# Neural-operator attention block on one core: scores in four column groups, grams in blocks, another row basis, softmax by batch, and pinned ends of the load stage

## The chip, the cores and the metric

The kernel runs on one core of a Trainium2 chip. The metric is device time in microseconds of that core for one execution. Before the change three runs gave 870.6, 871.68 and 877.57, median 871.68. One further execution was profiled and took 871.11; its recorded span is 869.6.

## The reference

The input x has 4 batches of 32 tokens; each token is an image of 128x128 fp32. The network has two layers. Layer 0 adds to x an attention over Fourier operators of the row-normalised x (`_L0_conv_ref`), then a recurrent scan; layer 1 is a resampling convolution and another scan. The change touches the start of layer 0 only:

```python
x = x + _L0_conv_ref(_ln_c(x), ...)
# in _L0_conv_ref: 16 heads; every token is one image
k = fno_layer(tokens_norm, key_w, key_skip_w, key_skip_b, (64, 64))
q = fno_layer(tokens_norm, query_w, query_skip_w, query_skip_b, (64, 64))
v = fno_layer(tokens_norm, value_w, value_skip_w, value_skip_b, (128, 128))
dprod = softmax(einsum('bhtd,bhsd->bhts', qf, kf) / scale, axis=-1)
attn = einsum('bhts,bhsd->bhtd', dprod, vf)
attn = fno_layer(attn, proj_w, proj_skip_w, proj_skip_b, (H, W))
```

`fno_layer` is a 1x1 convolution resampled through the Fourier domain plus a product with 16x9 (or 32x17) complex Fourier weights. Within a batch the scores are thus a sum of two parts: products of few Fourier coefficients with weights by head, and for all heads the same inner products of the images resampled to 64x64 (the grams), scaled by query_skip_w * key_skip_w of the head. Because attention is linear in v, the kernel mixes images with one 32x32 matrix per batch, and Fourier coefficients with the probabilities by head.

## The kernel before

All 128 images stand in on-chip memory as `XA`, 128 rows in the partitions, (batch, token, column) in the free dimension. The stage that loads and transforms them works in eight steps k of 16 images, two per batch.

- `stats(k, n)` takes mean and variance of each image row (L824, one instruction per image) and small vectors from them (L382 to L387, `rsqrt_of` with a square root on ACT, L830, L832). L833 fills `rv4`, from which the scale `s4` of a token's own norm comes later.
- `transform(k)` normalises the images in place (L846 on ACT for 10 of 16, L848 on DVE for 6), multiplies each with 130 constant columns (L863, `ps_st`, three images to a PSUM tile of which there are two), and copies the result to `A1` (L865 on DVE for the first and fourth of six groups, L867 on ACT for the others). Of the 130 columns 64 are a row Fourier transform and 66 resample the rows from 128 to 64: 64 real ones and two imaginary ones. Then come the column transform (L874, `ps_pf`, four groups of 32 output partitions) and the column resampling (L883, `ps_pr`, two groups of 64; the real and the imaginary part are each 512 wide), which ACT copies to `Rn` (L885). Last, L887 issues on SP the write of the 16 normalised images to a DRAM scratch, `normed`.
- `scores(b)` takes a batch's coefficients (L894 `FF`, L895 its transpose, L901 `ps_fr` copies them to all partition groups, L902 `Frep`), multiplies by head (L915, L929, L930 `KM`), transposes (L923 `ps_fq`, L937 `ps_kt`, copies L925 and L938) and multiplies (L941) into `psc`, batch b in partitions 32b to 32b+31, all 16 heads side by side in 512 columns.
- `grams(k)` (L951, `pg`) sums 32 products of 64x64 for two batches at once; of the result only the two diagonal 32x32 blocks are read (L1011).
- `weights()` and `filters()` prepare parameters; they are generators, as the others are, and a loop takes one step of each between two groups of `ps_st`. `filters` tests and stores the taps of layer 1's filters (L760 to L806 on DVE, L770 and L771 `ps_f` on PE, L749 and L808 write `hankel` in DRAM, which L1945 reads much later).

The loop over k (below) sets in which order the work is written out. Outside a block `in_order()` a planner may still place each engine's instructions otherwise; inside one, the order written is each engine's order.

After the loop, SP reads the scratch back with rows and images exchanged (L983, eight parts of 1 MB), and one softmax follows for all batches: `Pm` holds 16 heads x 32 tokens in 512 columns for the 128 (batch, token) partitions (L1022 to L1031), four transposes (L1035), scaling to `PTs` (L1036, L1038), and the sum over heads to the mixing matrix `CTbd` (L1044 to L1053). POOL clears `YT` (L1249).

The next stage is pinned by the list `SUMS`: F (L1261, `df`) multiplies coefficients on DVE, Y (L1274, `ps_y`) sums them with `PTs` on PE, M (L1067, `pm`) mixes images with `CTbd`.

## Time and profile before

| stretch (us) | what runs | length | PE busy | DVE busy | ACT busy |
|---|---|---|---|---|---|
| 20:40 | transforms 0 and 1, most input | 20 | 18.12 | 18.22 | 14.24 |
| 40:60 | transforms 2, 3, scores of batch 0 | 20 | 18.77 | 17.28 | 13.02 |
| 60:80 | transforms 3, 4, first grams | 20 | 19.66 | 18.57 | 13.77 |
| 80:100 | transforms 5, 6 | 20 | 18.86 | 13.09 | 12.83 |
| 130:140 | softmax | 10 | 2.13 | 8.89 | 1.26 |
| 140:150 | sums and mixing | 10 | 10.00 | 10.00 | 6.47 |

Time of the profiled execution 871.11, its span 869.6. Over the whole span PE is busy 88%, DVE 82%, ACT 74%, POOL 42%; the chain that ended last lies on PE for 39%, DVE 22%, ACT 13%.

To read it: a busy share says how long an engine had an instruction in flight. Matmul ends are modelled and overlap, so the share of PE is no measure of its speed. A releaser is what ended an engine's idle time. Engines are PE (matmul), PEld (its weight load), DVE (vector), ACT (scalar), POOL (GpSimd), SP (issues transfers).

### The profile page before, as it was taken

The page shows a single profiled execution, that of the slowest core. Times are in us where ns is not written, and L with a number is a line of the kernel's source. Part 1 is how long each engine was busy: PE and PEld are TensorE (multiplying, and loading weights), DVE is VectorE, ACT ScalarE, POOL GpSimd, SP SyncE. Part 2 cuts the span into 40 slices and gives each one's busy share as a digit, 9 for nine tenths or more (in the row PEclk, how much of TensorE's full clock was granted, in tenths as well). Part 3 has the DMA queues.
Part 4 walks back from the last instruction along what each step waited for, and adds up shares of the span by engine and source line. Part 5 has one row for each costly group of instructions (what it writes and reads, how often), then busy time and mean ns, then how long its engine had stood idle before and what let it go on. Part 6 is the DMA issues. An engine that isn't in the chain of part 4 may idle for free.

```text
span 869.6 us, 30563 instructions
## 1 busy us (share of the span) xinstructions
PE 762.7 (88%) x12326; PEld 559.4 (64%) x12326; DVE 712.0 (82%) x2322; ACT 640.2 (74%) x1647; POOL 364.2 (42%) x604
## 2 busy tenths in 40 slices
PE   1999996986878999899779979999999999998994
PEld 1656553335644655645339968888788887875993
DVE  5987749977588899899889988977868877678996
ACT  2765743585728698989779977877777887777994
POOL 2000000011435445364410016788788786972263
PEclk9999997996689899999999979999999999999997
DMA  9955991259711011120000000111111101118554
GB/s 216 265 159 116 256 368 68 101 220 265 191 50 49 26 44 31 49 73 26 25 1 1 1 3 17 41 41 39 29 40 28 41 28 41 35 44 288 175 197 137
DMA packets 105128, 83.18 MB, mean 96 GB/s; under 512 B 5457, under 2 KB 98129, under 8 KB 102865
## 3 DMA queue, kind: packets, MB, share of 16 engines
q1 hardware_dynamic: 104641, 80.86, 31.0%
q8 instruction: 99, 1.62, 0.8%
q0 software_dynamic: 288, 0.01, 0.2%
q14 instruction: 52, 0.43, 0.2%
q10 hardware_dynamic: 48, 0.26, 0.2%
HBM read 47.46 MB, written 33.66 MB: 93 GB/s over the span
## 4 chain that ended last, share of the span: by engine, by line
PE 39%; DVE 22%; ACT 13%; POOL 8%; issue 5%; SPq 0%; DVEq 0%; ACTq 0%; POOLq 0%
PE ps_k L2043 5%; PE ps_d L2173 4%; DVE XA L1562 4%; ACT WXY L1892 4%; DVE XA L1561 4%; PE ps_scan L1890 4%; ACT yw L1892 3%; PE pm L1067 3%; PE ps_st L1404 3%; PE ps_r L2043 2%; POOL XN L2022 2%; PE ps_e L2180 2%; PE ps_inv L488 2%; PE ps_y L1274 2%; PE ps_w L2119 2%
## 5 line engine op out<-in xcount | busy, mean ns | idle before, releaser
L2163 DVE SCALAR_TENSOR_TENSOR U<-raw 128x512 f32<-128x512 f32 x128 | 90.2, 733 | 27.7 <-ACT raw L2155 27.5
L1891 DVE SCALAR_TENSOR_TENSOR ps_scan<-WXY,bs,ps_scan 128x128 f32<-128x128 f32 x376 | 104.7, 351 | 1.2 <-PE ps_scan L1890 0.8
L2043 PE MATMUL ps_k<-WXY,q 64*64 64x134 f32 x2048 | 85.7, 280 | 1.3 <-issue 0.4
L2155 ACT COPY raw<-ps_k 128x512 f32<-128x512 f32 x128 | 71.2, 599 | 17.8 <-PE ps_k L2043 15.1
L2173 PEld LDWEIGHTS ps_d<-WXY,U 128*64 128x64 f32 x2048 | 66.7, 137 | 19.3 <-issue 11.4
L2022 POOL TENSOR_SCALAR XN<-XA,c_r,c_o 128x128 f32<-128x128 f32 x120 | 75.8, 642 | 4.7 <-issue 2.2
L2022 POOL TENSOR_SCALAR xn<-XA,f_r,f_o 128x128 f32<-128x128 f32 x120 | 68.3, 579 | 17.7 <-PE ps_x L2043 11.7
L2173 PE MATMUL ps_d<-WXY,U 128*64 128x67 f32 x2048 | 73.3, 224 | 1.2 <-ACT q L2186 0.9
L2043 PEld LDWEIGHTS ps_k<-WXY,q 64*64 64x64 f32 x2048 | 60.2, 134 | 7.1 <-DVE U L2163 0.8
L2043 PE MATMUL ps_r<-WXY,XN 64*64 64x134 f32 x1024 | 58.6, 287 | 3.0 <-DVE XN L2022 1.3
L863 PE MATMUL ps_st<-cst,XA 128*128 128x130 f32 x256 | 44.1, 310 | 16.6 <-ACT XA L846 13.0
L863 PEld LDWEIGHTS ps_st<-cst,XA 128*128 128x128 f32 x256 | 35.2, 204 | 30.3 <-ACT XA L846 14.4
L1619 ACT ACTIVATE xn<-XA,f_o,f_r 128x128 f32<-128x128 f32 x120 | 51.0, 489 | 4.6 <-DVE f_o L1601 3.4
L1398 ACT ACTIVATE Z<-Z,k,aB 128x128 f32<-128x128 f32 x128 | 51.1, 481 | 4.2 <-DVE Z L1393 4.0
L1561 DVE SCALAR_TENSOR_TENSOR XA<-ps_inv,r1B,xin 128x128 f32<-128x128 f32 x128 | 44.0, 344 | 8.2 <-PE ps_inv L1554 8.2
L1562 DVE SCALAR_TENSOR_TENSOR XA<-Z,gB,XA 128x128 f32<-128x128 f32 x128 | 46.3, 362 | 5.0
L2002 POOL TENSOR_TENSOR c_r<-c_e,neg_half 128x16 f32<-128x16 f32 (+2 forms) x10 | 25.7, 2565 | 52.9 <-DVE c_e L1995 52.7
L2141 ACT COPY q<-ps_r 128x512 f32<-128x512 f32 x64 | 38.3, 599 | 12.2 <-PE ps_r L2043 11.8
L503 PE MATMUL ps_inv<-invq,cst 64*128 64x512 f32 x128 | 41.4, 674 | 3.9 <-ACT invq L494 3.2
L453 PE MATMUL ps_wx<-xt,wvt 128*128 128x512 f32 x64 | 35.8, 643 | 6.5 <-ACT WXY L460 5.2
L2180 PE MATMUL ps_e<-WXY,q 128*64 128x67 f32 x1024 | 41.1, 222 | 0.0
L1890 PE MATMUL ps_scan<-y,wvt 128*128 128x128 f32 x246 | 40.5, 281 | 0.0
(442 smaller groups left out, 2102.4 us busy)
## 6 DMA issues: line engine op xcount, KB each, us to landing
XA<-in_x_dram SPq DMA_DIRECT2D x16, 512.0 KB, 7.5
normed<-XA SPq DMA_DIRECT2D x8, 1024.0 KB, 7.3
XA<-normed SPq DMA_DIRECT2D x8, 1024.0 KB, 16.0
mixed<-XA SPq DMA_DIRECT2D x8, 1024.0 KB, 3.9
XA<-mixed SPq DMA_DIRECT2D x32, 256.0 KB, 5.3
xin<-in_x_dram SPq DMA_DIRECT2D x32, 256.0 KB, 3.2
turned<-XA SPq DMA_DIRECT2D x32, 256.0 KB, 2.5
out_dram<-res SPq DMA_DIRECT2D x52, 128.0 KB, 2.1
```

Of the source, the lines that this page charges most:

```text
L863: mm(p[:, i, :], XA[:, b, t0 + j + i, :], cst[:, C_E : C_E + 130], start=True, stop=True)
L1561: stt(a, p2[c, b][:, i], r1B[:, j : j + 1], xin[c, b - b % 2][:, b % 2, i], ALU.mult, ALU.add)
L1562: stt(a, Z[c][:, b, i], gB[c][:, n : n + 1], a, ALU.mult, ALU.add)
L1890: mm(p4, self.t[:, 1, :], prev, start=True, stop=True)
L1891: stt(p4, WX[:, :, h, :], s[:, 0:1], p4, ALU.mult, ALU.add)
L1892: nc.scalar.activation(dst, p4, AF.Sigmoid, bias=s[:, 1:2])
L2022: e.tensor_scalar(dst, src_, r, o, ALU.mult, ALU.add)
L2043: m = mm(dst, data, taps, start=(n == 0 and (i, j) not in last), stop=(n == 1), skip_group_check=True)
L2155: nc.scalar.copy(raw[u, k], banks["k", u][:, k])
L2163: stt(U[u][:, k].rearrange("p k s m -> p (k s m)"), v, SLOPE, v, ALU.mult, ALU.max)
L2173: mm(p[HALVES[s], m, b, REACH[k]], U[v][:, b, k, s, HALVES[m]], DR[:, k, REACH[k]], start=(m == 0 and b == 0 and k == 0), stop=(k == 1), s ...
L2180: mm(p[HALVES[j], b * P : b * P + P][:, REACH[m]], q3[v - 1][:, m, b, HALVES[j]], DC[:, m, REACH[m]], start=(b == 0 and m == 0), stop=(m = ...
```

## The change

1. The 64 real columns that resample rows are multiplied by an orthogonal matrix (even and odd rows, then cosines and sines), and so are the two imaginary ones, of which only the first two columns are then in use. Grams don't depend on the basis. The imaginary part becomes one matmul of 32 columns into the lower half.
2. `A1` is copied by ACT alone.
3. `psc` holds partitions (group of four heads is in the columns, key side) as [group g, token] by [batch, head in group, token]: each of the three products is cut in four matmuls of 128 columns to the four groups of 32 partitions. Probabilities of one batch are then 128 partitions x 128 columns.
4. `gram(b)` replaces `grams(k)`: for each batch 32 matmuls of 32x32 in four groups, copied once and summed over the groups and spread to all of them by one matmul with `rep4`.
5. `scales()` and `attend(b)` replace the softmax after the loop; `softmax` steps are taken in transforms 6 and 7 for batches 0 to 2, and `attend(3)` follows at the end. The mixing matrix of a batch comes from four matmuls of `heads` with `PTs`.
6. The first two transforms, and the last scores with the last gram and the filters, stand in `in_order()` blocks. The steps of `filters` (`extra`), taken in transforms 5 to 7 before, are all in the last block or right after it in the same block, ahead of `attend(3)`.

The diff, cut to its core:

```diff
-    c[:, C_E + 64 : C_E + 128] = rows.real.T
-    c[:, C_E + 128 : C_E + 130] = rows.imag.T[:, :2]
+    turn = 2 * np.pi * np.outer(h2, np.arange(1, 32)) / 64
+    basis = np.concatenate([(h2[:, None] % 2 == np.arange(2)) / np.sqrt(32), np.cos(turn) / np.sqrt(32),
+                            np.sin(turn) / np.sqrt(32)], 1)
+    c[:, C_E + 64 : C_E + 128] = rows.real.T @ basis
+    c[:, C_E + 128 : C_E + 130] = (rows.imag.T @ basis)[:, :2]
...
-    psc = ps1.tile([P, NH, NT], F32, name="psc")
+    psc = ps1.tile([P, NB, 4, NT], F32, name="psc")
...
-                if n % 3 == 0:
-                    nc.vector.tensor_copy(A1[:, j : j + m, :], p[:, :m])
-                else:
-                    nc.scalar.copy(A1[:, j : j + m, :], p[:, :m])
+                nc.scalar.copy(A1[:, j : j + m, :], p[:, :m])
...
-            for part in range(2):
-
-                for half in range(2):
-                    q = slice(64 * half, 64 * half + 64)
-                    a = (A1[:, :, 64 + 32 * half : 96 + 32 * half] if part == 0 else
-                         A1[:, :, 128:130].unsqueeze(2).broadcast_to([P, HB, 16, 2]))
-                    mm(p[q], cst[:, C_CR + 64 * part : C_CR + 64 * part + 64], a, start=(part == 0), stop=(part == 1))
+            for half in range(2):
+                mm(p[64 * half : 64 * half + 64], cst[:, C_CR : C_CR + 64], A1[:, :, 64 + 32 * half : 96 + 32 * half],
+                   start=True, stop=True)
+            mm(p[0:64, :, 0:2], cst[:, C_CR + 64 : C_CR + 128], A1[:, :, 128:130], start=False, stop=True,
+               skip_group_check=True)
...
             for k in range(3):
-                mm(psc[32 * b : 32 * b + 32].rearrange("p h s -> p (h s)"), FQ[:, k, :],
-                   KT[:, k].rearrange("p g n -> p (g n)"), start=(k == 0), stop=(k == 2))
+                for g in range(4):
+                    mm(psc[32 * g : 32 * g + 32, b].rearrange("p q s -> p (q s)"), FQ[:, k, :], KT[:, k, g],
+                       start=(k == 0), stop=(k == 2))
...
+        def gram(b):
+
+            q = slice(32 * b, 32 * b + 32)
+            for i in range(8):
+                for g in range(4):
+                    mm(pg[32 * g : 32 * g + 32, b], Rn[:, 8 * g + i, q], Rn[:, 8 * g + i, q],
+                       start=(i == 0), stop=(i == 7))
+            part = sp.tile([P, NT], F32, tag="part", name="part")
+            nc.scalar.copy(part, pg[:, b])
+            yield True
+            mm(pg[:, 4 + b], rep4.rearrange("p a t -> p (a t)"), part, start=True, stop=True)
+            yield True
...
+        def attend(b):
...
+            tt(Pm, by_head(wqk), by_token(pg[:, 4 + b]), ALU.mult)
+            tt(Pm, Pm, psc[:, b], ALU.add)
+            tt(Pm, Pm, by_token(sTL[:, b]), ALU.mult)
+            nc.vector.tensor_reduce(mx, Pm, AX.X, ALU.max)
+            tt(Pm, Pm, by_head(mx), ALU.subtract)
+            yield True
+            nc.scalar.activation(Pm, Pm, AF.Exp)
+            nc.vector.tensor_reduce(mx, Pm, AX.X, ALU.add)
+            nc.vector.reciprocal(mx, mx)
+            tt(Pm, Pm, by_head(mx), ALU.mult)
+            yield True
+            p = big("ps_pt")[:, :P]
+            nc.tensor.transpose(p, Pm.rearrange("p q s -> p (q s)"), ident)
+            ts(PTs[:, 0, b], p, s4[:, b : b + 1], None, ALU.mult)
+            nc.scalar.mul(PTs[:, 1, b], PTs[:, 0, b], -1.0)
+            yield True
+            q = slice(32 * b, 32 * b + 32)
+            for g in range(4):
+                mm(pg[q, 8], heads[:, g], PTs[:, 0, b, 32 * g : 32 * g + 32], start=(g == 0), stop=(g == 3))
+            tt(CTbd[q, q], pg[q, 8], cst[q, C_ID : C_ID + 32], ALU.add)
+            yield True
...
+        with in_order():
+            through(stats(0, 1))
+            ahead = stats(1, 1)
+            for n, _ in enumerate(transform(0)):
+                step(prepare if n == 1 else ahead if n > 1 else None)
+            through(ahead)
+            ahead = stats(2, 2)
+            for _ in transform(1):
+                step(ahead)
+        scoring = attention(0)
+        next(scoring)
+        for k in range(2, 2 * NB):
...
             for _ in transform(k):
-                for other in (ahead, prepare if k > 2 else None, before, halfway if k == 5 else None, extra if k > 4 else None):
-                    if other is not None:
-                        next(other, None)
+                step(ahead, prepare if k > 2 else None, scoring, softmax if k > 5 else None)
             if k % 2 == 1:
-                for _ in before or ():
-                    pass
-                before = scores(k // 2)
-                next(before)
+                through(scoring)
+                scoring = attention(k // 2) if k < 2 * NB - 1 else scores(k // 2)
+                if k < 2 * NB - 1:
+                    next(scoring)
...
+        through(softmax, prepare)
+        products = gram(NB - 1)
+        with in_order():
+            for work in (scoring, extra, extra, extra, scoring, scoring, scoring, products, products, scoring, scoring,
+                         scoring, scoring, scoring, extra, extra, scoring):
+                step(work)
+            through(scoring, extra, attend(NB - 1))
```

`through` runs generators to their end, `step` takes one step of each, and `attention(b)` is `scores(b)` followed by `gram(b)`. `scales()` computes `s4`, the scales `sTL` of the scores, `wqk` (query times key skip weight / 64) and `heads` (proj times value skip weight on a 32x32 identity, per group), and ends with an exponential that loads ACT's table. In the sums, `PTs` is read as [batch, group] instead of [group, batch].

## The prediction

> **What bounds the kernel now.** First the granted clock and span of the core (0.951, 869.6 us), then the table of busy time by stretches, then groups by line, then the timeline of the stretch where the change lies. The first 139 us are the part that the diff touches: x comes in, eight transforms `transform(k)` of 16 images each, four `scores(b)`, the grams, one softmax. The chain of waits is complete from 113.6 us on, and runs through the Fourier products, scores and softmax into the mixing. Everything after 138.9 us is the same code, and starts later or earlier as a whole.
>
> Columns: stretch, length, busy PE, PEld, DVE, ACT, POOL, clock, DMA share, GB/s. The first three are pairs of transforms (2,3), (4,5), (6,7), cut where `ps_pr` starts; the fourth is the end of the stage.
>
> ```profile
> 37.47:63.63 26.16, 24.66 (x172) 14.97 (x168) 22.51 (x90) 18.67 (x47) 0.96 (x3) 0.93 0.74 185
> 63.63:92.69 29.06, 28.18 (x218) 17.37 (x214) 22.78 (x116) 16.20 (x40) 0.00 (x0) 1.00 0.63 132
> 92.69:114.64 21.95, 20.60 (x142) 12.03 (x140) 10.61 (x36) 14.28 (x34) 0.63 (x1) 1.00 0.85 255
> 113.64:138.90 25.26, 17.00 (x131) 10.81 (x131) 15.84 (x39) 8.84 (x19) 0.90 (x1) 0.81 0.71 299
> ```
>
> The reader is to see PE at 94 to 97% in the pairs, with DVE close behind in the first two (86%, 78%), and ACT at 71, 56 and 65%. PE's share overstates (ends are modelled), but between 104.34 and 114.64 its queue has no hole: its rows add up to 10.3 us of 10.3. So PE is the bound, DVE second, and ACT has room.
>
> In the groups of the first 160 us (count, busy, mean ns, then what ended the idle time before them):
>
> ```profile
> L883 PE MATMUL ps_pr<-A,cst 128*64 128x512 f32 x64 | 15.6, 608 | 0.0
> L941 PE MATMUL psc<-KT,FQ 96*32 96x512 f32 x24 | 11.8, 600 | 0.0
> L951 PE MATMUL pg<-WXY 128*64 128x64 f32 x128 | 10.7, 245 | 0.0
> L867 ACT COPY A<-ps_st 128x390 f32<-128x390 f32 x24 | 11.7, 486 | 15.2 <-PE ps_st L863 14.9
> L865 DVE COPY A<-ps_st 128x390 f32<-128x390 f32 x16 | 8.9, 556 | 12.8 <-PE ps_st L863 12.8
> L1261 DVE TENSOR_TENSOR df<-WXY 128x1088 f32<-128x1088 f32 x18 | 21.7, 1282 | 0.0
> ```
>
> Two records stand for one fp32 matmul. The first three rows are what the change cuts on PE; L865 goes to ACT. From the timeline:
>
> ```profile
> 74.79 1.07 PE L874 MATMUL ps_pf<-A,cst 128*32 128x256 f32 x16
> 104.34 1.94 PE L883 MATMUL ps_pr<-A,cst 128*64 128x512 f32 x8
> 110.19 3.99 SPq L983 DMA_DIRECT2D XA<-normed  x8
> 119.57 5.26 PE L951 MATMUL pg<-WXY 128*64 128x64 f32 x64
> 127.80 1.90 PE L941 MATMUL psc<-KT,FQ 96*32 96x512 f32 x4
> 129.74 0.69 DVE L1023 TENSOR_TENSOR Pm<-Pm,psc 128x512 f32<-128x512 f32 x1 [1.64 <-PE psc L941]
> 138.89 7.30 DVE L1261 TENSOR_TENSOR df<-WXY 128x1088 f32<-128x1088 f32 x6
> ```
>
> The last line is the mark: the next stage is a full DVE (10.00 busy of 10 in 140:150), so its first `df` at 138.89 sets the rest.
>
> **What the Trainium skill says.** "TensorEngine Tiling (Array Packing)", Theoretical Speedup: outputs of at most 32 columns can run four side by side. The trace agrees: 16 `ps_pf` records in 1.07 us are 67 ns each, against about 240 ns for a 512-wide record of `ps_pr` of which two share the array. "TensorE: Matmul & The Clock Gate", LDWEIGHTS: loading goes by columns of the weight; here a load takes 204 ns (128 columns), 138 (64) and 109 (32). "VectorE: DVE Perf Modes", section on the errata: a fp32 tensor_tensor takes (N+151)/0.96 ns, 691 for 512; the trace has 689 to 693, and 273 where the formula gives 291 (N = 128). "ScalarE: Activation LUTs", What ACT_TABLE_LOAD costs: 186 + 0.833 N ns for an activation and 1283 ns for a table load; the trace has 630 (612 by formula) and 1283.
>
> **The change, part by part.**
>
> *Rows in another basis.* `ps_pr` falls from 8 records of 512 (1.94 us) to 4 plus 2 of 32 columns: about 0.97 + 0.1. Eight times 0.87 = 7 us of PE work, 5.2 in the six transforms from 37.5 on.
>
> *Scores by column groups.* 6 records of 512 one after the other (1.90 + 1.04 - overlap = 2.8 us) become 24 of 128 columns, four abreast: 24 x 107 ns / 4 = 0.65, with loads about 0.8. Saves 2 us of PE per batch.
>
> *Grams in blocks.* Not shown before. 64 records per batch instead of 64 per two. If weight loads bound them, 37 ns (`ps_pf` loads, 16 in 0.59) to 52 ns (`ps_y`, 32 in 1.66), 2.4 to 3.3 us per batch; if they don't run abreast, 82 ns as now, 5.3. I take 3.2. Three are in the loop (9.6 us, was 5.3), the last lies in the end beside DVE's products.
>
> *Evacuation.* 16 DVE copies (8.9 us) become ACT's, 16 x 0.486 = 7.8, of which 5.9 in the pairs. I price it by what is then the wait, inside the loop below; its cover is ACT's idle time (7.5, 12.9 and 7.7 us in the pairs), and with none of it the loop would gain nothing.
>
> *Filters.* Some 50 small DVE instructions and four `ps_f` matmuls leave the loop (about 5 us of DVE; PE's waits of 0.4 for them too) for the pinned end. `hankel<-fzero` moves on SP behind the eight readbacks, `hankel<-taps` on POOL behind it, and the `YT` memset (L1249) waits behind that on POOL; its first reader is at 184 us and hankel's is later, so I price this at nothing.
>
> *Softmax by batch.* `scales` and three `attend` minus their last steps go into transforms 6 and 7, where DVE is busy 10.6 of 21.95: some 35 instructions of 0.2 to 0.27, 8 us at most, hidden there; PE +1.5 us with the s4 products (1.05 now in the end).
>
> **Loop.** PE per pair after: (2,3) 26.2 - 1.7 - 2 + 3.2 = 25.7 by PE, but its DVE loses 2.2 and the waits of DVE on `ps_st` go (12.8 us in all, 5 outside the end): 24.5. (4,5): 29.1 - 1.7 - 2 - 5.3 + 3.2 - 1 (waits for the filters), plus 1 for ACT in its place: 23.5. (6,7): 22 - 1.7 - 2 + 3.2 + 2 = 23.5. Sum 71.5 instead of 77.2: **-5.7 us**. ACT then has 10 x 0.41 + 2.7 + 1.03 + 2.3 = 10.1 us per transform, 20.3 per pair, 86% of 23.5.
>
> **Start.** Transform 0 began at 18.55 since its statistics were interleaved with the second chunk's; pinned, it can begin near 12.7 (two chunks read by 10.3, then twelve small steps). But the statistics of batch 1 and the first step of `weights` (3.5 us of DVE) now lie between, and DVE has 25.5 us of work from 6.2 on before transform 2, which began at 36.6. I take **-1 us**, bounds +2 and -4.
>
> **End.** To the last KM add (124.61) nothing moves: s4's products go (-1), but the pinned `ps_f` of the filters stands on PE ahead of `ps_fr` and waits for DVE (+1). Transposes start 0.3 earlier without the 64 grams in front; `psc` ends at 127.4 instead of 129.7. Then DVE must finish the filters before `attend(3)`, in pinned order: 14 dependent steps of about 0.15, and a PE result that comes after `psc`: +2.5 (bounds 0 and 3.5). The softmax, 9.15 us from 129.74 to 138.89, shrinks with its width: five DVE steps of 0.30, exp 0.34, sum, reciprocal and product 0.82, transpose 0.48, scaling 0.32, four small matmuls 0.45, add 0.2: 4.1. The table load (1.28) leaves the end. 127.4 + 2.5 + 4.1 = 134.0 for the first `df`: **-4.9 us**.
>
> The readback (L983) starts after the last write of `normed` and moves 8 MB at some 420 GB/s until 131; the first mixing needs one eighth of it, and later ones come each 7 us, so it is not next in line.
>
> Sum -11.6 on the profiled execution's 871.1 (span 869.6 and 1.5 around it), which lies 0.6 below the median 871.7 of the three runs: 859.5 to 860.1. **860 us**.
>
> **Rivals.** *ACT takes PE's place (slower).* In no pair was ACT over 71% busy, and it works in order: a copy that waits for `ps_st` holds the normalisations that PE waits for next. At 71% its 20.3 us need 28.6 per pair, 86 in all: +8.6, and 876 with the other two gains; at 65% 94, and 884. It decides from 83.1 us for the three pairs on (77.2 + 4.9 + 1): 27.7 per pair, ACT under 73%. For it: L867 already waits 14.9 for `ps_st`. Against: at the 37-50 us window ACT did 11.37 of 13.06, 87%. Chance 0.14.
>
> *The loop gains nothing:* blocks that don't overlap (+2.1 per batch) or ACT waits eat it, and only the end and start gain: 866, between 862 and 870. Chance 0.18.
>
> *PE's floor:* the pairs go to PE's pure work, 20.7, 20.7, 22.5 = 64 (-13), the filters hide under the score copies (-2 more), start -2: 850. Chance 0.10.
>
> *My forecast:* 0.58, own range 853 to 865.
>
> **From these to the numbers.** Half of the slow rival and the low edge of the third case are left out: 851 to 873 holds about 8 in 10. One per cent, about what can be told from no change here, is 8.7 us: below 863 lie four fifths of the forecast, the third case and a little of the second, plus some weight for costs priced high: 0.64; above 880.4 part of the first rival: 0.08; between them 0.28.
>
> **What would show it.** `ps_pr` near 1.1 us per transform; `psc` under 1 us a batch; grams at 50 ns a record; pairs near 24 us with ACT over 80% busy; first `df` near 127, `attend(3)` near 4 us behind a filter step. Wrong if pairs pass 27 us with PE waiting for ACT, if grams stay at 82 ns, or if the pinned start puts transform 2 later than 38 us.

## The result, and the profile after

Twenty runs of the changed kernel have the median 871.28 us (868.74 to 875.70); twenty of the kernel before beside them 871.86. The ratio is 0.9983, 95% interval 0.9965 to 1.0001: no difference that can be told. The profiled execution took 870.38, its span is 868.6 (before 871.11 and 869.6).

The first `df`, the mark at which the unchanged part begins, comes at 136.80 instead of 138.89. That small sum hides three large ones. Read from the start of `ps_pr` in each transform:

| stretch | before | after | predicted |
|---|---|---|---|
| start to `ps_pr` of transform 1 | 37.48 | 43.06 (**+5.6**) | -1 |
| transforms 2 to 7 | 77.2 | 68.4 (**-8.8**) | -5.7 |
| last `ps_pr` to first `df` | 24.25 | 25.34 (**+1.1**) | -4.9 |

First the table of busy time by stretches of the kernel after (stretch, length, busy PE, PEld, DVE, ACT, POOL, clock, DMA share, GB/s): the three pairs of transforms, the end, and the two tens of us in which the end lies.

```profile
43.06:68.14 25.08, 22.28 (x251) 15.93 (x248) 22.52 (x97) 21.00 (x54) 0.68 (x3) 1.00 0.54 151
68.14:88.65 20.51, 18.64 (x223) 13.35 (x219) 20.33 (x98) 18.08 (x45) 0.00 (x0) 1.00 0.49 99
88.65:111.46 22.81, 20.59 (x245) 14.98 (x241) 13.13 (x41) 19.14 (x48) 0.00 (x0) 1.00 0.94 253
111.46:136.80 25.34, 13.47 (x156) 8.30 (x153) 16.05 (x70) 6.94 (x16) 1.46 (x2) 0.61 0.81 332
120.00:130.00 10.00, 6.53 (x112) 5.11 (x109) 6.65 (x25) 3.14 (x8) 0.00 (x0) 0.50 1.02 428
130.00:140.00 10.00, 4.26 (x13) 2.20 (x14) 7.75 (x26) 1.64 (x5) 1.46 (x2) 0.50 0.31 129
```

PE is down from 94 to 97% of the pairs to 89 to 91%; ACT is up to 84 to 88%. DVE has lost its copies and yet is up to 90 and 99% in the first two pairs (86 and 78% before), since these are shorter. The gain is almost all in the pair (4,5), 29.06 before. In the end PE is busy for 13.5 us, in the kernel before for 16.0 between the same marks (the prediction's 17.0 begins 1 us earlier), and the stretch is no shorter: it consists of waits. The clock granted to it is 0.61, and half from 120 us on.

Next the groups by line of the kernel after, first 160 us (count, busy, mean ns, then the idle time before them and what ended it).

```profile
L863 ACT COPY A<-ps_st 128x390 f32<-128x390 f32 x40 | 19.1, 483 | 8.8 <-PE ps_st L862 8.3
L870 PE MATMUL ps_pf<-A,cst 128*32 128x256 f32 x128 | 11.3, 417 | 3.9 <-ACT A L863 3.9
L874 PE MATMUL ps_pr<-A,cst 128*64 128x512 f32 x32 | 9.9, 629 | 0.0
L936 PE MATMUL psc<-KT,FQ 96*32 96x128 f32 x96 | 4.5, 313 | 0.0
L947 PE MATMUL pg<-WXY 128*32 128x32 f32 x256 | 4.2, 210 | 0.0
```

The three cuts on PE are there: `ps_pr` 15.6 to 9.9 us (and 2.1 for the small third matmul), `psc` 11.8 to 4.5, grams 10.7 to 4.2. A mean per record says little where four records run side by side; the timeline gives the length. Timeline of the kernel after (start, length, engine, operation, then the idle time before it and what ended it), start and end of the stage:

```profile
12.07 0.17 DVE L379 TENSOR_TENSOR rq_d<-rq_d,rq_e 128x16 f32<-128x16 f32 x1
17.07 0.15 DVE L717 TENSOR_SCALAR ndcm<-cst 128x1 f32<-128x1 f32 x1 [4.82 <-DMA cst<-in_consts_dram]
17.14 0.28 DVE L380 SCALAR_TENSOR_TENSOR p_r<-rq_d,p_r 128x16 f32<-128x16 f32 x1
18.22 2.97 PE L862 MATMUL ps_st<-cst,XA 128*128 128x130 f32 x12 [18.22 <-ACT XA L845]
...
22.62 0.16 DVE L644 TENSOR_TENSOR QK<-QK,mQK 128x2 f32<-128x2 f32 x1 [3.87 <-ACT mQK L666]
25.63 3.40 PE L862 MATMUL ps_st<-cst,XA 128*128 128x130 f32 x14 [2.38 <-DVE XA L847]
35.37 6.34 PE L862 MATMUL ps_st<-cst,XA 128*128 128x130 f32 x32 [2.77 <-ACT XA L845]
...
104.31 0.86 PE L936 MATMUL psc<-KT,FQ 96*32 96x128 f32 x24
106.20 0.76 PE L947 MATMUL pg<-WXY 128*32 128x32 f32 x64
...
112.72 0.71 DVE L889 STREAM_TRANSPOSE FF<-FF 128x512 f32<-128x512 f32 x1 [1.36 <-ACT FF L888]
116.59 0.33 PE L1013 MATMUL ps_pt<-ident,Pm 128*128 128x128 f32 x1 [2.69 <-DVE Pm L1010]
116.85 0.21 PE L769 MATMUL ps_f<-fsq,ones_sq 7*7 7x24 f32 x2
117.03 1.27 PE L895 MATMUL ps_fr<-FF,WXY 32*128 32x272 f32 x2
124.88 0.75 DVE L924 TENSOR_TENSOR KM<-KM,WXY 128x576 f32<-128x576 f32 x1
125.11 2.76 PE L931 MATMUL ps_kt<-ident,KM 128*96 128x128 f32 x12 [2.65 <-DVE KM L923]
127.81 1.51 PE L936 MATMUL psc<-KT,FQ 96*32 96x128 f32 x24
129.57 0.18 DVE L772 COPY sums<-ps_f 7x38 f32<-7x38 f32 x1 [2.26 <-PE ps_f L770]
132.10 0.27 DVE L1001 TENSOR_TENSOR Pm<-wqk,pg 128x128 f32<-128x128 f32 x1
136.80 1.29 DVE L1286 TENSOR_TENSOR df<-WXY 128x1088 f32<-128x1088 f32 x1
```

In the kernel before, where the last `ps_pr` begins at 114.64, `ps_fr` and the last KM add stand here:

```profile
117.49 1.06 PE L901 MATMUL ps_fr<-FF,WXY 32*128 32x272 f32 x6
123.86 0.75 DVE L930 TENSOR_TENSOR KM<-KM,WXY 128x576 f32<-128x576 f32 x1
```

Three things are to be seen. **At the start** one small instruction, `ndcm`, stands on DVE in the middle of the first square root chain. It belongs to `weights` and is read only at 68.2 us (in the kernel before it ran at 59.9); the planner placed it there, outside what the block pins. It reads the second part of the constants, which land at 17 us, and DVE, which takes its instructions in the order of its queue, stands for 4.82 us. Then DVE waits for `QK`, and PE for DVE's normalisations. **At the end** `ps_fr` begins at 117.03 although its input is transposed by 113.4: on PE the leftover transpose of `attend(2)` and the filters' `ps_f` stand ahead of it, the first of them waiting for DVE. And `attend(3)` begins at 132.10 although `psc` is done at 129.3: the filters' small steps on DVE from 129.57 on, 2.5 us, stand between, the first of them waiting 2.26 us for a `ps_f` that PE has behind `psc`. **In between**, 64 gram records take 0.76 us, 12 ns each.

### The profile page after: what moved, and what is told of

Its sections match the earlier page's. It is cut to its first block, busy times and chain, and to the rows that moved or that the text cites. A ratio compares the mean times of both kernels' runs of the same rounds, so it can differ in the third digit from the quotient of the medians.

```text
span 868.6 us, 31057 instructions
## 1 busy us (share of the span) xinstructions
PE 750.8 (86%) x12550; PEld 560.5 (65%) x12550; DVE 710.9 (82%) x2330; ACT 649.4 (75%) x1669; POOL 361.2 (42%) x604
## 4 chain that ended last, share of the span: by engine, by line
PE 44%; DVE 25%; ACT 14%; POOL 9%; issue 5%; DMA 1%; SPq 1%; DVEq 0%; ACTq 0%; POOLq 0%
PE ps_k L2068 5%; PE ps_scan L1915 4%; DVE XA L1587 4%; PE ps_d L2198 4%; ACT WXY L1917 4%; DVE XA L1586 4%; PE ps_st L862 3%; ACT yw L1917 3%; POOL XN L2047 3%; PE pm L1092 3%; PE ps_st L1429 3%; PE ps_r L2068 2%; PE ps_e L2205 2%; PE ps_y L1299 2%; POOL xn L2047 2%
## 5 line engine op out<-in xcount | busy, mean ns | idle before, releaser
L2180 ACT COPY raw<-ps_k 128x512 f32<-128x512 f32 x128 | 71.0, 597 | 17.0 <-PE ps_k L2068 14.6
L845 ACT ACTIVATE XA<-XA,p_n,p_r 128x128 f32<-128x128 f32 x80 | 35.4, 491 | 7.6 <-DVE p_n L829 7.6
```

The lines of the kernel that those rows point to most:

```text
L2180: nc.scalar.copy(raw[u, k], banks["k", u][:, k])
```

## The experiments

All edits are to the changed kernel unless said otherwise. The ratio is to runs of the kernel before on the same chip (the changed kernel has 0.9983 by this measure); the three stretches are those of the table above, from each profiled execution; the clock is the one granted in 40:60. e3, e12 and e14 rest on four executions each, e10, e11 and e13 on five, the others on 11 to 20.

| run | ratio, interval | to `ps_pr` of 1 | 2 to 7 | end | clock |
|---|---|---|---|---|---|
| before | 1 | 37.48 | 77.2 | 24.25 | 0.91 |
| after | 0.9983 (0.9965, 1.0001) | 43.06 | 68.4 | 25.34 | 1.00 |
| e1 | 0.9925 (0.9897, 0.9954) | 37.27 | 73.5 | 24.55 | 0.66 |
| e2 | 0.9968 (0.9948, 0.9988) | 43.20 | 71.7 | 21.11 | 1.00 |
| e3 | 0.9893 (0.9827, 0.9959) | 36.25 | 67.4 | 25.53 | 1.00 |
| e4 | 1.0067 (1.0045, 1.0090) | 42.67 | 74.3 | 24.95 | 0.83 |
| e5 | 0.9979 (0.9960, 0.9998) | 42.77 | 69.5 | 22.88 | 0.91 |
| e6 | 1.0036 (1.0018, 1.0054) | 41.78 | 68.4 | 28.26 | 1.00 |
| e7 | 0.9977 (0.9960, 0.9994) | 41.89 | 71.7 | 25.52 | 0.74 |
| e8 | 1.0032 (1.0010, 1.0054) | 43.45 | 72.5 | 24.98 | 1.00 |
| e9 | 0.9994 (0.9974, 1.0014) | 43.66 | 68.8 | 25.47 | 1.00 |
| e10 | 0.9914 (0.9886, 0.9942) | 36.57 | 71.9 | 24.42 | 1.00 |
| e11 | 0.9897 (0.9860, 0.9933) | 42.19 | 73.8 | 18.91 | 0.74 |
| e12 | 0.9857 (0.9822, 0.9892) | 36.49 | 72.3 | 18.14 | 1.00 |
| e13 | 0.9895 (0.9869, 0.9921) | 36.77 | 72.0 | 23.30 | 1.00 |
| e14 | 0.9810 (0.9766, 0.9855) | 35.42 | 70.0 | 18.86 | 1.00 |

The last column matters. In the profiled executions of e1, e7 and e11 PE's clock is halved for 10 to 14 us between 42 and 57, and the loop of that one execution is then 3 to 5 us longer than the changed kernel's; so where the column is under 1, the ratio over many runs is a better witness than the one profile. The profiled executions of e11 (871.16) and e13 (871.54) were also the slowest of their five. The column doesn't show all of it: in e10 and e12 the half clock comes just behind its stretch, for 6.8 us from 60.1 on, and in e14 for 3.4 us from 63.0 and again from 86.9 on. The loops of the changed kernel, e3, e6, e8 and e13 ran at full clock.

### The start

**e1: `ndcm` on POOL**, so that DVE's chain isn't cut.

```diff
-        ts(ndcm, dcm, -1.0, 1.0, ALU.mult, ALU.add)
+        nc.gpsimd.tensor_scalar(ndcm, dcm, -1.0, 1.0, ALU.mult, ALU.add)
```

> The changed kernel with one instruction moved: ndcm (one column from the second part of the constants) is computed by POOL instead of DVE. In the changed kernel DVE stood 4.8 us in front of it, in the middle of the first statistics, until those constants had landed. Theory A (the start gave the gain away): first transform begins near 12.8 instead of 17.7, first df near 132.5, time 4 to 5 us below the changed kernel, ratio to the kernel before 0.993. Theory B (the start is bound by the arrival of x, or a later fixed point swallows it): first df stays within 1 us of 136.8, ratio 0.998.

Measured: the first `ps_st` at 13.28 instead of 18.22, `ps_pr` of transform 1 at 37.27 instead of 43.06, ratio 0.9925, median 865.84. The intervals of e1 and of the changed kernel don't meet. One instruction of 0.15 us cost about 5 us. The start of PE in e1:

```profile
13.28 2.97 PE L862 MATMUL ps_st<-cst,XA 128*128 128x130 f32 x12 [13.28 <-ACT XA L845]
```

In its profiled execution much of the gain was lost again before transform 2, to the clock, as the table by stretches of e1 shows (the clock is the third number from the right):

```profile
42.00:56.00 14.00, 13.51 (x67) 9.93 (x69) 14.00 (x50) 9.13 (x25) 1.81 (x3) 0.52 0.96 260
```

PE is 96% busy there at half clock, and from `ps_pr` of transform 1 to that of transform 2 it takes 18.6 us instead of 13.5 in the changed kernel.

**e3: the first two transforms as before**, outside a pinned block and with the old order of their steps.

```diff
-        with in_order():
-            through(stats(0, 1))
-            ahead = stats(1, 1)
-            for n, _ in enumerate(transform(0)):
-                step(prepare if n == 1 else ahead if n > 1 else None)
-            through(ahead)
-            ahead = stats(2, 2)
-            for _ in transform(1):
-                step(ahead)
+        through(stats(0, 1))
+        next(prepare)
+        through(stats(1, 1))
+        ahead = None
+        for k in range(2):
+            if k == 0:
+                ahead = stats(2, 2)
+            for _ in transform(k):
+                step(ahead)
```

> The changed kernel with the first two transforms written out as in the kernel before, without a pinned order. Theory A (the pinned start cost 5.6 us up to the second ps_pr): second ps_pr back from 43.1 to 37.5, first df near 131, ratio 0.992. Theory B (the loop gained what the start lost, since work was only pushed from one into the other): the six later transforms take 74 us instead of 68 and the ratio stays 0.998.

Measured: `ps_pr` of transform 1 at 36.25, the loop and the end as in the changed kernel (67.4 and 25.5), first `df` at 129.14, ratio 0.9893. PE starts six microseconds later than in e1 (19.11) and is through transform 1 a microsecond sooner: the early start that the pinned block buys is spent between its transforms. Within their intervals e1 and e3 are worth the same.

**e10: the pinned start in another order**, statistics of the second chunk first, then the first step of `weights`; `ndcm` on POOL as in e1.

```diff
-                step(prepare if n == 1 else ahead if n > 1 else None)
-            through(ahead)
+                step(ahead if n < 5 else None)
+            through(ahead)
+            next(prepare)
```

> ndcm is computed on POOL, and in the pinned start the statistics of the second chunk are taken in the first five steps of transform 0, the first step of weights after them instead of ahead of them. If the start lost its time to that order (DVE waits 4.5 us for QK with the statistics of transform 1 behind it, and PE waits between the transforms), ps_pr of k = 1 comes at 30 to 33 us (37.3 with ndcm alone on POOL, 43.1 in the changed kernel), k = 2 at 44 to 47, and the median is 858 to 862. Rival, x comes in too late or DVE's own work sets the start: k = 2 not before 50, median 865 or more.

Measured: transform 0 ends early (`ps_pr` at 22.32, 26.04 in e1), but transform 1 comes at 36.57, only 0.7 before e1's, and transform 2 at 50.45; ratio 0.9914, median 865.29. The main expectation failed, its rival (x comes in too late) holds. The timeline of e10 on DVE:

```profile
19.87 0.17 DVE L375 TENSOR_SCALAR rq_e<-p_v 128x16 f32<-128x16 f32 x1
24.22 0.87 DVE L823 BATCH_NORM_STATS2 st<-XA 128x6 f32<-128x128 f32 x4 [4.18 <-DMA XA<-in_x_dram]
25.01 0.23 DVE L377 RECIPROCAL p_r<-rq_q 128x16 f32<-128x16 f32 x1
```

The same pattern as with `ndcm`: the planner put four statistics of a later batch, written behind the block, into the middle of the second chunk's square root chain, and their input lands at 24.2. What waits on DVE changes from the constants to `QK` to x; transform 1 stays at 36 to 37.

### The end

**e2: the filters' steps back in transforms 5 to 7.**

```diff
-                step(ahead, prepare if k > 2 else None, scoring, softmax if k > 5 else None)
+                step(ahead, prepare if k > 2 else None, scoring, softmax if k > 5 else None, extra if k > 4 else None)
...
-        through(softmax, prepare)
+        through(softmax, prepare, extra)
...
-            for work in (scoring, extra, extra, extra, scoring, scoring, scoring, products, products, scoring, scoring,
-                         scoring, scoring, scoring, extra, extra, scoring):
+            for work in (scoring, scoring, scoring, scoring, products, products, scoring, scoring,
+                         scoring, scoring, scoring, scoring):
```

> The changed kernel with the filters' steps taken in transforms 5 to 7 again and not in the pinned end. Theory A (they hold the last softmax by 2.8 us and ps_fr by less): from the last ps_pr to the first df 22 instead of 25.3, the loop longer by 1 to 2, ratio 0.996. Theory B (they only fill waiting time there, and what holds the end is PE at half clock and the softmax of batch 2): end 24.5 to 25, loop longer by 2, ratio 0.999 to 1.000.

Measured: the end falls by 4.2 us to 21.11, the loop grows by 3.3. Ratio 0.9968; the interval overlaps that of the changed kernel. The filters do cost the end four microseconds, but the loop asks for most of them again: 1.1, 1.6 and 0.6 us in transforms 5, 6 and 7.

**e5: another order of the pinned end**, with the last steps of `attend(2)` and the first `ps_f` behind `ps_fr`, the second `ps_f` ahead of `psc`.

```diff
-        through(softmax, prepare)
+        through(prepare)
...
-            for work in (scoring, extra, extra, extra, scoring, scoring, scoring, products, products, scoring, scoring,
-                         scoring, scoring, scoring, extra, extra, scoring):
+            for work in (scoring, softmax, extra, scoring, scoring, extra, scoring, products, products, scoring, scoring,
+                         softmax, extra, scoring, scoring, scoring, softmax, extra, extra, extra, scoring):
                 step(work)
-            through(scoring, extra, attend(NB - 1))
+            through(scoring, extra, softmax, attend(NB - 1))
```

> The pinned end is written in another order: the last steps of attend(2) (transpose, four small matmuls) and the filters' first ps_f stand behind the four ps_fr on PE, and the filters' second ps_f stands ahead of psc instead of behind it. No instruction is added or removed. If the end lost its gain to the order (ps_fr at 117.0 although FF was transposed at 113.4; attend(3) 2.8 us behind psc), ps_fr begins within 1 us of the transpose, first df comes 3 to 5 us after fewer microseconds from the last ps_pr (25.3 falls to 20.5 to 22.5), and the median is 866 to 868.5. Rival, the clock: PE at half clock in 120:140 sets the end and what is gained ahead of it is waited out by DVE later: the end stays over 24 us and the median within 1 us of the changed kernel's 871.

Measured: `ps_fr` follows 0.4 us behind the transpose, the end is 22.88, 2.5 less, a little short of what the first theory asked; in the median, 869.38, it doesn't show: ratio 0.9979 against 0.9983. The filters still stood between the last products and `attend(3)` on DVE until 130.4.

**e11: that order, with the filters in transform 7**, where DVE has the least to do.

```diff
-                step(ahead, prepare if k > 2 else None, scoring, softmax if k > 5 else None)
+                step(ahead, prepare if k > 2 else None, scoring, softmax if k > 5 else None, extra if k > 6 else None)
...
+            for work in (scoring, softmax, scoring, scoring, scoring, products, products, scoring, scoring, softmax,
+                         extra, extra, scoring, scoring, scoring, softmax, scoring):
```

> The end is in the order of the run e5 (attend(2)'s last steps behind ps_fr), and the filters' steps are taken in transform 7, where DVE is busy 3.8 of 10.7 us, instead of the pinned end. If the filters on DVE between psc and attend(3) and between the last KM products cost what the end lacks, the last ps_pr to first df falls from 25.3 (22.9 in e5) to 19 to 20.5, transform 7 stays within 1 us, and the median is 865 to 867. Rival: transform 7 pays for the filters (as the loop did by 3.3 us where they were taken in transforms 5 to 7), and the median is over 868.

Measured: the end is 18.91 instead of 25.34, transform 7 takes 11.2 us instead of 10.7, and the ratio is 0.9897, median 864.88. The loop of the profiled execution is long for its clock, not for the filters: 3.5 of its 5.4 us more lie between transforms 1 and 2. Timeline of e11, end of the stage:

```profile
117.20 0.71 DVE L889 STREAM_TRANSPOSE FF<-FF 128x512 f32<-128x512 f32 x1 [1.16 <-ACT FF L888]
118.31 0.73 PE L895 MATMUL ps_fr<-FF,WXY 32*128 32x272 f32 x4
125.79 2.77 PE L931 MATMUL ps_kt<-ident,KM 128*96 128x128 f32 x12 [1.67 <-DVE KM L923]
129.43 0.29 DVE L1001 TENSOR_TENSOR Pm<-wqk,pg 128x128 f32<-128x128 f32 x1
130.46 0.29 DVE L1002 TENSOR_TENSOR Pm<-Pm,psc 128x128 f32<-128x128 f32 x1 [0.74 <-PE psc L936]
134.85 1.29 DVE L1286 TENSOR_TENSOR df<-WXY 128x1088 f32<-128x1088 f32 x1
```

Now `attend(3)` starts ahead of the end of `psc` and its second instruction waits for nothing but `psc`. The end takes 5.3 us less than in the kernel before, where 4.9 were predicted. That the two agree is luck: the 4.9 had already paid 2.5 us for filters ahead of `attend(3)`, and these are gone here, so that the prediction's own terms ask for 7.4. The 2 us that lack lie mostly between the last KM add and the end of `psc`, 4.1 us where it had 2.8, with `ps_kt` at 2.77 us.

**e6: PE kept busy in the end** by matmuls whose results nobody reads.

```diff
+        def warm(n):
+            for _ in range(n):
+                mm(pg[:, 10:14].rearrange("p a t -> p (a t)"), ident, cst[:, 0:128], start=True, stop=True)
+            yield True
...
+            for work in (scoring, extra, extra, extra, scoring, scoring, scoring, warm(8), products, products, scoring,
+                         warm(8), scoring, scoring, scoring, scoring, extra, extra, scoring, warm(8)):
+                step(work)
+            through(scoring, extra)
+            for work in attend(NB - 1):
+                through(warm(2))
```

> Matmuls of 128 columns whose results nobody reads are put on PE into the stretches of the pinned end in which it waits (8 behind ps_fr, 8 behind the last gram, 8 behind psc, two after each step of attend(3)), nothing else. If the low granted clock of 120:140 (0.50) comes from PE standing idle and costs the end time, the clock there rises over 0.8, three ps_kt fall from 2.76 to about 1.6 us and psc from 1.5 to 0.9, and first df comes about 2 us earlier: median 869. Rival, the end is a matter of order and DVE alone: clock may rise, but first df stays within 0.7 us or comes later behind the added matmuls; median 870.5 to 873.

Measured, in the table by stretches of e6:

```profile
120.00:130.00 10.00, 9.62 (x146) 8.41 (x145) 5.79 (x19) 1.97 (x5) 0.00 (x0) 0.88 1.01 423
```

The clock rises from 0.50 to 0.88 and the three `ps_kt` fall from 2.76 to 1.47 us, so in this stretch PE has more of its clock when it is kept busy. But the added matmuls stand ahead of the grams, of `ps_kt` and of the second `ps_f`, which DVE then awaits for 4.79 us; the end grows to 28.26 and the ratio to 1.0036. What a warm PE would be worth without that stays open.

### The loop

**e13: the kernel before with one part of the change**, the copies of `A1` on ACT alone.

```diff
-                if n % 3 == 0:
-                    nc.vector.tensor_copy(A1[:, j : j + m, :], p[:, :m])
-                else:
-                    nc.scalar.copy(A1[:, j : j + m, :], p[:, :m])
+                nc.scalar.copy(A1[:, j : j + m, :], p[:, :m])
```

> The kernel before with one part of the change alone: ACT makes all copies of A1. If PE bounded the kernel before, as its 94 to 97% in the pairs of transforms said, its work is the same here and little is gained: the pairs fall from 77.2 to 75 to 77 us and the median to 869.5 to 872, and the 5.9 us that this part is worth in the changed kernel exist only since PE's work was cut. If the copies on DVE were a bound of their own, the pairs fall to 71 to 73 us here too and the median to 866 to 867. If ACT takes PE's place (the prediction's slow rival), the pairs grow past 79 us.

Measured: ratio 0.9895, median 865.38, pairs 72.0: the second theory's numbers, the median a little under them. This one edit, alone, beats the whole change. Its table by stretches, cut as those shown of before and after:

```profile
36.77:61.10 24.33, 23.43 (x172) 14.51 (x168) 21.44 (x92) 22.46 (x59) 3.67 (x3) 1.00 0.80 203
61.10:87.34 26.24, 25.77 (x218) 16.72 (x214) 21.43 (x116) 16.83 (x42) 0.00 (x0) 1.00 0.55 114
87.34:108.78 21.44, 20.20 (x143) 11.96 (x140) 6.00 (x15) 13.82 (x33) 0.56 (x1) 1.00 0.92 249
```

With the same work on PE the pairs fall by 1.8, 2.8 and 0.5 us, 5.1 in all; PE stays at 94 to 98% busy throughout. The first pair of the kernel before ran 3.4 us at half clock (0.93 in the mean, 1.00 here), so up to 1.7 us of its 1.8, half of that stretch, may be clock (an estimate); the second has 1.00 in both. There the same 218 records are busy for 28.18 us before and 25.77 here. So that share before was no proof that PE's own work filled the time: part of a record's busy time was waiting. ACT reaches 92% in the first pair, and the pair is shorter all the same.

**e4: the reverse**, the copies shared with DVE again in the changed kernel (the edit of e13 backwards).

> The changed kernel with the copies of ps_st shared again, DVE two of six and ACT four. Theory A (DVE was the second bound, ACT has room): pairs of transforms longer by 2 each, ratio 1.003. Theory B (ACT at 84 to 86 per cent is now the bound of the pairs): pairs shorter by 1 to 2 each, ratio 0.993.

Measured: ratio 1.0067, median 876.98; loop 74.3. By pairs the rise is +6.4, +0.7 and -1.2, so all of it is in the first, which this execution ran at clock 0.84. The twenty runs say that the part is worth some 0.84% of the time; how much of this is DVE's copies and how much the clock, one profile can't say. It is nearly twice what the first theory had (1.003). With everything changed but the copies, the loop is thus 2.9 us under the kernel before; with the copies alone (e13) 5.1; with both 8.8.

**e7: two of ten normalisations from ACT to POOL; e9: four of six from DVE to POOL**, in transforms 2 to 7.

```diff
-                if i % 8 not in (1, 4, 6):
+                if k > 1 and i % 8 == 7:
+                    nc.gpsimd.tensor_scalar(u, u, r[:, i : i + 1], nmr[:, i : i + 1], ALU.mult, ALU.add)
+                elif i % 8 not in (1, 4, 6):
```

```diff
-                if i % 8 not in (1, 4, 6):
+                if k > 1 and i % 8 in (1, 4):
+                    nc.gpsimd.tensor_scalar(u, u, r[:, i : i + 1], nmr[:, i : i + 1], ALU.mult, ALU.add)
+                elif i % 8 not in (1, 4, 6):
```

> In transforms 2 to 7, two of the ten images that ACT normalises are normalised by POOL, which is idle there. If ACT (86% busy, full in 65:80) is what bounds the loop since it makes all copies of A1, each transform loses 0.8 us of ACT and the six of them 3 to 5 us: k = 2 to 7 falls from 68.4 to 64 to 66, median 867 to 868. Rival, DVE or PE bounds it: 68.4 stays within 1 us. A second rival: POOL's instruction takes over 1.5 us or slows DVE, and the loop grows by over 1 us.

> In transforms 2 to 7, four of the six images that DVE normalises are normalised by POOL (0.53 us each there). Nothing else is changed. If DVE (18.6 of 20 us busy in 40:80) is what bounds the pairs (2,3) and (4,5) now that ACT's relief brought nothing, each of these four transforms loses about 1.2 us: k = 2 to 7 falls from 68.4 to 64 to 66 us and the median to 866 to 868. Rival, PE with its chain through ps_st, copy and ps_pf bounds it (the doubled ps_pr cost 4 us): 68.4 stays within 1 us. If POOL's instruction slows DVE, the loop grows.

Measured: neither helps. e7 has the ratio 0.9977; its loop is longer between transforms 1 and 2 at the low clock, and from transform 2 to 7 it takes 54.85 us, the changed kernel 54.88. e9 has 0.9994 and a loop of 68.8; by pairs that is 1.6 less, 0.6 more and 1.3 more, the last at clock 0.93. POOL takes longer for a normalisation, 0.54 us in e7 and 0.57 in e9, against 0.49 on ACT and 0.34 on DVE. Over the whole loop neither ACT at 84 to 88% nor DVE at 90 to 99% is the bound by itself; for DVE in the pair (2,3) e9 leaves it open.

**e8: the two wide matmuls of `ps_pr` issued twice**, so that it takes 1.94 us again.

```diff
-            for half in range(2):
+            for half in (0, 1, 0, 1):
```

> The two 512 wide matmuls of ps_pr are issued twice with the same result, so that ps_pr takes 1.94 us a transform again, as it did in the old basis, and nothing else is changed. If PE still bounds the loop, each transform grows by 0.87 us, k = 2 to 7 from 68.4 to 73 to 74 us, and the median is 876 or more. If ACT and DVE bound it since the copies moved (PE's rows are short of the stretch), the loop grows by under 2 us and the median stays under 873: the saving that the prediction counts at 5.2 us was then mostly not on the path.

Measured: the loop grows by 4.1 us and the ratio by 0.5%, of 6 x 0.87 = 5.2 added. That lies between its two theories, nearer the first: with the copies moved, PE's added work is paid for in every pair (1.3, 1.6 and 1.2 us), at four fifths of its price.

### Both ends mended

**e12: e10's start with e11's end.** **e14: e3's start with e11's end.**

> The start of e10 and the end of e11 together. If the two losses are the whole of what the prediction missed and they are independent, the gains add: median 853 to 858, first df at 120 to 126. Rival: what the start gains is waited out in the loop, or the input and the readback, which then meet, hold the end: median over 860.

> The start of e3 (the first two transforms as in the kernel before) with the end of e11 (filters in transform 7, attend(2)'s last steps behind ps_fr). If the two losses are independent, their gains add: e3's 6.4 and e11's 6 to 8 us below the changed kernel, median 857 to 859.5, first df at 122 to 125. Rival: it is not under e12's 860.9, since the clock in the end is low and the readback holds it.

Measured: 860.85, ratio 0.9857, and 858.62, ratio 0.9810; first `df` at 126.96 and 124.23. e12 misses its expected 853 to 858 by 3 us, on the side of its rival: its loop takes 72.3 us, 3.9 more than that of the changed kernel. 6.8 us of it are at half clock, and whether the rest is start waited out, as the rival says, the one profile can't tell. e14 lies inside its own. The ratios of e3 and e11 together promise 1.76% under the changed kernel, and e14 has 1.73; those of e10 and e11 promise 1.55, and e12 has 1.26. With four executions each both agree with gains that add, and e14 says so the more clearly. e14 is the fastest here, 1.9% (1.5 to 2.3) under the kernel before, and needs no operation that the change did not bring.

## Why the prediction was wrong

The forecast of 860 fails by 11 us, on the side that it gave as its second rival ("The loop gains nothing", 866) and past it; but not for that rival's reason. By its own steps:

- **Loop, predicted -5.7, measured -8.8.** The loop gained, but largely not by the steps of the sum: two errors partly cancel, and that it comes out on the right side is in part luck. The first is the step "So PE is the bound, DVE second, and ACT has room". It took PE's busy share for PE's need, from the last ten microseconds of the last pair; even there PE is busy for 9.86 us of 10.30, not all of them, with 0.44 us of waiting for a copy of ACT. From this step the sum gives the copies 1.2 us in the pair (2,3) and takes 1 back for ACT in (4,5). e13 shows 5.1 us for them (up to 1.7 of it clock) with no cut on PE at all: 1.8 and 2.8 in these two pairs, and 0.5 in the last, from which the step was read. The second is the grams' term, 3.2 us per batch (50 ns a record), which measured 0.76: 7.3 us too dear over three batches. With that term right the step's sum would have been -13.0, and 4.2 us of it did not come. e13 leaves 3.6 us for all cuts on PE and the softmax together, and no run takes these apart. `ps_pr` at 1.08 + 0.25 (1.07 predicted) and `psc` at 0.86 (0.8) were sized well. By pairs, predicted 24.5, 23.5 and 23.5 (the terms written for the second add up to 23.3), measured 25.1, 20.5 and 22.8; with the grams right, the first lacks 3.0 us and the last 1.7. The first is 22.6 in e3 (and the second 22.0), so most of what it lacks goes with the pinned start. What else holds the pairs stays open: e8 says that PE's work is still paid for at four fifths, e7 and e9 that neither ACT nor DVE is the whole of it.
- **Start, predicted -1 with bounds +2 and -4, measured +5.6.** This step failed first. "Pinned, it can begin near 12.7" was right for the pinned instructions (13.28 in e1), but the step took the block for the whole of DVE's queue. An instruction written outside the block was placed inside it, with an input from a transfer that lands at 17 us. e1 removes it and finds 37.27, -0.2 against before. That is still not the -1: in e1 PE begins 5.8 us earlier than in the kernel before, but the order written in the block makes DVE wait 4.5 us for `QK`, and transform 2 begins at 41.6 us, not at 36.6.
- **End, predicted -4.9, measured +1.1.** Taken apart: to the last KM add nothing was to move, and it takes 4.2 us longer (14.2 instead of 10.0 from the last `ps_pr`); the gain to the end of `psc` is 1.4, not 2.3, with `psc` and `ps_kt` at half clock; filters in front of `attend(3)` 2.8 (2.5 predicted); `attend(3)` itself 4.7 instead of 9.15 (4.1 predicted). The failed step is "To the last KM add (124.61) nothing moves". It priced `ps_f` ahead of `ps_fr` (+1), but not that three steps of `attend(2)` were left when the loop ended (14 steps are taken in transforms 6 and 7, of 17), so that its transpose stood on PE ahead of `ps_fr` and waited for a softmax on DVE. The four small matmuls behind that transpose also stand between the first and the second half of `ps_fr`. With these moved (e5) the last KM add comes 10.5 us behind the last `ps_pr` again; with the filters out of the end as well (e11) the end is 5.3 us shorter than in the kernel before.
- **Rival "ACT takes PE's place".** Refuted: the longest pair is 25.1 us, far from the 27.7 at which that rival decides, and relief of ACT brings nothing (e7). (By its own terms its times are about 874 and 882, not 876 and 884.)
- **"PE's floor", 64 us for the pairs.** Not reached in any run; 67.4 (e3) is the shortest.
- **The sign against it** did appear: the pinned start put transform 2 later than 38 us (first normalisation at 47.4, and at 41.6 in e1). Its cause was not among the rivals.

The sum is made by start and end: +6.6 and +6.0 against the steps, -3.1 from the loop. Mended, the kernel stands at 858.6, close to the forecast; but that is two errors removed, not the forecast confirmed. At the first `df` e14 leads by 14.7 us, where the steps said 11.6, and it loses five of them later.

What is not settled: a gain at the first `df` isn't wholly kept. In e13's profiled execution the lead is 6.8 us at 206 us and gone at 814; in e14's 14.6 and 9.0; in the changed kernel's own 2.1 and 0.2. The code there is the same in all of them. e13's four other executions, at 864.6 to 865.4, must have kept theirs by their times, though no profile shows them. What takes it away was not tried.

## What to carry to other kernels

Where an order is pinned by hand, list what may still enter the queue from outside it: one instruction of 0.15 us whose input is still in flight can stop an engine that works in order for five, and it is found as a line with a transfer as its releaser in a chain that has no business with transfers. Count how many steps a generator has left where a loop ends; they become the head of what follows. And test a busy PE by taking a copy away from its consumers before believing its share: if the time falls with PE's work unchanged, part of the share was waiting.

## What the runs showed of the hardware

**PE's clock and the scatter of the runs.** Over 168 runs of 14 kernels, each kernel's own mean taken out, the time goes with the mean granted clock with a correlation of -0.84: 0.01 less clock goes with 4.7 us more. Which of the two brings the other, the runs don't say. The changed kernel has a mean of 0.941, the kernel before 0.950 (46 runs), though part of the low clock falls where PE has nothing to do. The Trainium skill, "TensorE: Matmul & The Clock Gate", What's actually happening, has the clock halved after an idle window of about 3.4 us and full after a busy one, on a window that runs freely. These traces agree in the kind: 0.50 and 1.00 in nearly all short stretches, and the rate of `ps_kt` halved with it (2.76 and 1.47 us for the same twelve matmuls). One thing differs: in e1 the half clock lasts for some 14 us from 42 us on, although PE's records fill 13.51 of the 14.00 us, where the page has the full clock back after one busy window. What is counted as busy for the clock isn't shown by these records.

**Grams.** The same page, Wait — 56ns, not 53.3ns?, says that matmuls of 32 columns start at least 25 ns apart. Here 64 records of 32 columns take 0.76 us, 12 ns each at full clock and 17 (1.08 us) at half. They go to four groups of output partitions; in each of these 16 records make 48 ns each, so the page's figure is not contradicted for one group, and the gain is that four groups run side by side. Their 64 weight loads take 0.65 us in all. The prediction's 50 ns, taken from weight loads of other operations in the trace, was four times too dear.
